# Group averages of the first norm: two matmuls with an averaging matrix, or block transposes and sums on VectorE

## Chip, cores and metric

The kernel runs on one core of a Trainium2 chip. The metric is the device time in microseconds (us) of one execution. Engines are named as in the profile: PE is TensorE (its weight loads are PEld), DVE is VectorE, ACT is ScalarE, POOL is GpSimd, and SP issues the DMAs.

## What is computed

The input is 32 images of 56 x 56 positions with 128 channels, float32. Two residual layers follow one another, each behind a group norm with 32 groups of four channels. Layer 0 is shifted-window attention (windows of 7 x 7, four heads), layer 1 a pair of truncated cosine transforms with a mixing matrix per mode and a feed-forward network (128 to 512 to 128).

```
def _gn(v, G=32, eps=1e-5):
    g = v.reshape(B_, H_, W_, G, C_ // G)
    m = mean(g, axis=(1, 2, 4));  s = var(g, axis=(1, 2, 4))
    return ((g - m) / sqrt(s + eps)).reshape(v.shape)

x = x + attention(_gn(x), rpb_table, w_qkv, w_proj, b_proj)
x = x + fourier_ff(_gn(x), w0, w1, W1, b1, W2, b2)
```

The change concerns the first `_gn` only. Its mean and variance run over all positions of an image and over the four channels of a group.

## The kernel before

Channels lie on the 128 partitions for the attention. An image is eight rows of windows (NWR = 8), and a row is one "cycle" of the main loop; a cycle takes about 14 us, an image about 112.5 us. Within a cycle the program issues, one after the other and in an order written by hand (`full_first`, then `quarters`, `attn_max`, `half_columns`, `eighths`, `full_last`), the pieces of three images: a row of attention of the present image, and the cosine transforms and the feed-forward groups of the one or two before. PE, ACT, DVE and POOL each execute their instructions strictly in that order; DMAs are issued by SP.

The statistics of the next image are prepared while the present one is still in attention. In cycles 4 to 6 of an image `next_image` calls `image_group` for the eight rows of the next image: PE transposes (L259), ACT copies the row (L269), DVE takes its per-channel statistics (L270), POOL adds the projection's bias to the residual (L274). After the three groups of cycle 6, `image_norm` starts. It is a generator that is advanced at four points: at the end of cycle 6, inside `full_first` of cycle 7, at the start of `full_last` of cycle 7, and at its end.

- Step 1: DVE aggregates mean and variance per channel (L281, `mv`).
- Step 2: PE multiplies the means by `gavg`, a 128 x 128 matrix with 0.25 in blocks of 4 x 4 (L284). DVE copies the group mean (L286), stores its negative as an extra column of the image's first row (L288), and forms e = (mean - group mean)^2 + variance (L290, L292).
- Step 3: PE averages e with the same matrix (L297), DVE adds 1e-5 (L299), POOL takes the power -1/2 (L301, `rstd`), DVE forms nb = -mean x rstd (L303).
- Step 4: ACT scales the projection weights by rstd (L308, `wn`), PE computes the bias of v (L310) and DVE copies it (L312). The next image's q and k matmuls (L321, L328) use `wn`.

Other lines that the text below speaks of: L429 copies half of the transposed attention weights from PSUM (DVE; the other half L427 is on ACT); L494 adds the projection to the residual and L508 and L517 sum it for the second norm (DVE); L333 on ACT and then L341 on DVE write the two halves of k for the scores L375 (PE); L405, L407 and L408 sum, invert and scale the softmax (DVE, DVE, POOL), L393, L394 and L400 take the maximum, subtract it and apply the exponential (DVE, POOL, ACT); L711, L719 and L731 are the feed-forward network (PE, ACT, PE), L701 adds its bias to the residual (POOL) and L740 adds the result (DVE). PSUM tiles of the attention rotate through four banks (`pa`), those of the second layer through four others (`pc`).

The part of `full_first` that sets the order around the second step of the norm:

```
attn_qk(im, i, False)          # L321, L328, then k on ACT and DVE
...
next(norm)                     # step 2
...
ff_in(im, FF_AT.index(c))      # L701, L711, L719
...
attn_divide(cycle - 1)         # L405, L407, L408
```

Of the kernel before, what the change touches and what calls it, by code (L numbers as in the profile page):

```python
# [10 lines left out]
F32 = mybir.dt.float32  # L11
AF = mybir.ActivationFunctionType
ALU = mybir.AluOpType
AX = mybir.AxisListType

P = 128
S = 56
C = 128
# [30 lines left out]
def swin_fourier_kernel(  # L49
# [20 lines left out]
    nc = tc.nc  # L70
    NB = x.shape[0]

    const = ctx.enter_context(tc.tile_pool(name="const", bufs=1))
    big = ctx.enter_context(tc.tile_pool(name="big", bufs=1))
    work = ctx.enter_context(tc.tile_pool(name="work", bufs=2))
    small = ctx.enter_context(tc.tile_pool(name="small", bufs=4))
# [3 lines left out]
    def bank(tag, bufs):  # L80
        return psum.tile([P, HB], F32, tag=tag, name=tag, bufs=bufs)

    def attn_bank():
        return bank("pa", 4)
# [38 lines left out]
    def const_load(shape, src, name):  # L123
        t = const.tile(shape, F32, tag=name, name=name)
        (nc.scalar if name in FIRST else nc.sync).dma_start(t, src)
        return t
# [9 lines left out]
    gavg = const_load([P, P], group_avg, "gavg")  # L136
# [11 lines left out]
    with nc.allow_non_contiguous_dma(reason="relative position bias, once"):  # L148
# [4 lines left out]
        for ix in range(WS):  # L153
            src = bass.AP(
                rpb_rev.tensor, rpb_rev.offset + WS - 1 - ix, [[span, NH * span], [1, WS]]
            )
# [41 lines left out]
    with nc.allow_non_contiguous_dma(reason="constant, once"):  # L198
        for blk in range(8):
# [4 lines left out]
            src = idct_h.rearrange("p (h r) -> p h r", r=4)[modes, :, 2 * li : 2 * li + 2]  # L204
# [47 lines left out]
    def image_group(im, i):  # L252
# [22 lines left out]
            piece, piece, bproj.unsqueeze(1).to_broadcast([TC, n1 - n0, C]), ALU.add  # L275
        )

    def image_norm(im):

        mv = small.tile([P, 2], F32, tag="mv", name="mv")  # L280
        nc.vector.bn_aggr(mv, im.st)  # L281
        yield
        pg = attn_bank()
        nc.tensor.matmul(pg[:, 0:1], lhsT=gavg, rhs=mv[:, 0:1], start=True, stop=True)  # L284
        gm = small.tile([P, 1], F32, tag="gm", name="gm")
        nc.vector.tensor_copy(gm, pg[:, 0:1])  # L286

        nc.vector.tensor_scalar(im.xw[0][:, RT : RT + 1], gm, -1.0, None, ALU.mult)  # L288
        d = small.tile([P, 1], F32, tag="d", name="d")
        nc.vector.tensor_tensor(d, mv[:, 0:1], gm, ALU.subtract)  # L290
        e = small.tile([P, 1], F32, tag="e", name="e")
        nc.vector.scalar_tensor_tensor(  # L292
            out=e, in0=d, scalar=d, in1=mv[:, 1:2], op0=ALU.mult, op1=ALU.add
        )
        yield
        pv = attn_bank()
        nc.tensor.matmul(pv[:, 0:1], lhsT=gavg, rhs=e, start=True, stop=True)  # L297
        ve = small.tile([P, 1], F32, tag="ve", name="ve")
        nc.vector.tensor_scalar(ve, pv[:, 0:1], 1e-5, None, ALU.add)  # L299
        rstd = small.tile([P, 1], F32, tag="rstd0", name="rstd0")  # L300
        nc.gpsimd.tensor_tensor(rstd, ve, mhalf, ALU.pow)  # L301
        nb = small.tile([P, 1], F32, tag="nb0", name="nb0")
        nc.vector.scalar_tensor_tensor(  # L303
            out=nb, in0=gm, scalar=-1.0, in1=rstd, op0=ALU.mult, op1=ALU.mult
        )
        im.w = work.tile([P, 3 * C], F32, tag="wn", name="wn")
        yield
        nc.scalar.mul(im.w, wqkv, rstd)  # L308
        pb = attn_bank()
        nc.tensor.matmul(pb[:, 0:1], lhsT=wqkv[:, 2 * C :], rhs=nb, start=True, stop=True)  # L310
        im.bias = small.tile([P, 5], F32, tag="bqkv", name="bqkv")
        nc.vector.tensor_copy(im.bias[:, 2:3], pb[:, 0:1])  # L312
        yield


# [597 lines left out]
    with tc.manual_schedule(engines={ET.PE, ET.Activation, ET.DVE, ET.Pool}):  # L913
        images[0] = image_begin(0)
        for i in range(NWR):
            image_group(images[0], i)
        for _ in image_norm(images[0]):
            pass
        norm = nothing()
        for cycle in range(NB * NWR + CONV_BEGIN + FF_AT[-1] - NWR + 1):  # L920
            if cycle < CONV_BEGIN:
                first_rows(cycle, norm)
            else:
                full_first(cycle, norm)
                if (cycle - CONV_BEGIN) % NWR != 3:
                    quarters(cycle)
                    if row(cycle)[0]:
                        attn_max(cycle)
                    half_columns(cycle)
                    eighths(cycle)  # L930
                else:
                    half_columns(cycle)
                    quarters(cycle)
                    eighths(cycle)
                    if row(cycle)[0]:
                        attn_max(cycle)
                full_last(cycle, norm)
            b, i = divmod(cycle, NWR)
            norm = nothing()
            if i == NWR - 2 and b + 1 < NB:  # L940
                norm = image_norm(images[b + 1])
                next(norm)
# [62 lines left out]
```

## Time and profile before

Three runs took 3694.38, 3694.4 and 3697.74 us.

| Engine or resource | Busy us | Share |
|---|---|---|
| PE | 3628.2 | 98% |
| PEld (overlaps PE) | 2966.3 | 80% |
| DVE | 2185.3 | 59% |
| ACT | 2151.0 | 58% |
| POOL | 1372.0 | 37% |
| DMA queue of SP | - | 37.6% of 16 engines |

The instructions of the norm, 32 times each (mean of one, in ns): L281 364, L286 150, L288 154, L290 181, L292 243, L299 150, L303 1120, L312 149 on DVE; L301 551 on POOL; L308 620 on ACT. A float32 matmul appears as two passes in the records, so L284, L297 and L310 have 64 entries each, of 214, 263 and 218 ns.

How to read it: PE's matmuls are pipelined and the records model their ends, so a busy PE need not be PE at its peak. A group's idle column tells how long its engine stood still just before it, and what released it. The timeline is in order of time and has the start, the duration and, in brackets, the idle time ahead.

### The profile page before, as it was taken

Reading aid. Unit: us, or ns where it says so; the run is one execution under the profiler, and the core shown is the slowest. Engines: PE = TensorE matmul, PEld = TensorE weight load, DVE = VectorE, ACT = ScalarE, POOL = GpSimd, SP = SyncE. Lnnn points to the kernel's source line nnn. Section 1 sums busy time; section 2 is a strip of 40 time slices with the busy share of each in tenths; the row PEclk is TensorE's granted clock in tenths of the full one; section 3 lists DMA queues with packets and bytes.
Section 4 is the critical chain, followed back from the end, with each engine's and each line's share of the span. In section 5 each row is a group of like instructions: output and inputs, shape, how many; then the busy total and the mean of one; then the engine's idle time right before and its main releaser. Section 6 shows DMA issues by size and latency. Waiting matters only on the chain.

```text
span 3694.8 us, 139935 instructions
## 1 busy us (share of the span) xinstructions
PE 3628.2 (98%) x61440; PEld 2966.3 (80%) x61440; DVE 2185.3 (59%) x4577; ACT 2151.0 (58%) x3915; POOL 1372.0 (37%) x1421
## 2 busy tenths in 40 slices
PE   6899999999999999999999999999999999999998
PEld 5678888888888887888888888878888888888886
DVE  6655666655665556665556656556655566565641
ACT  4555566655656655566556566555665565565553
POOL 5333343333334333433333343334333333433321
PEclk9999999999999999999999999999999999999999
DMA  4333434343434334334334344343344343333332
GB/s 112 93 102 104 116 93 109 107 111 101 113 95 114 108 105 113 96 105 110 108 102 113 95 111 108 105 113 100 101 112 108 101 115 97 108 107 106 95 107 89
DMA packets 687777, 388.93 MB, mean 105 GB/s; under 512 B 40479, under 2 KB 658112, under 8 KB 686912
## 3 DMA queue, kind: packets, MB, share of 16 engines
q1 hardware_dynamic: 686557, 379.65, 37.6%
q8 instruction: 484, 7.93, 0.9%
q14 instruction: 125, 1.02, 0.1%
q10 hardware_dynamic: 611, 0.32, 0.0%
HBM read 218.29 MB, written 161.48 MB: 103 GB/s over the span
## 4 chain that ended last, share of the span: by engine, by line
PE 93%; DVE 4%; DMA 1%; SPq 1%; ACT 1%; issue 0%; POOL 0%; ACTq 0%; POOLq 0%; DVEq 0%
PE pc L731 21%; PE pc L711 18%; PE pa L353 7%; PE pc L629 6%; PE pc L595 6%; PE pa L375 6%; PE pa L419 5%; PE pa L486 5%; PE pc L668 5%; PE pa L328 5%; PE pa L444 4%; PE pa L321 4%; PE pa L259 2%; DVE st L270 1%; DVE a L383 1%; DVE mx L393 1%
## 5 line engine op out<-in xcount | busy, mean ns | idle before, releaser
L408 POOL TENSOR_TENSOR a<-a,rs 128x784 f32<-128x784 f32 x256 | 389.9, 1523 | 1231.0 <-DVE rs L407 962.6
L731 PE MATMUL pc<-wff,hid 128*128 128x128 f32 (+1 forms) x6400 | 778.6, 279 | 0.9 <-ACT hid L719 0.7
L731 PEld LDWEIGHTS pc<-wff,hid 128*128 128x128 f32 (+1 forms) x6400 | 731.1, 189 | 21.1 <-issue 2.1
L711 PE MATMUL pc<-xf,wff 128*128 128x512 f32 (+2 forms) x1792 | 713.1, 540 | 0.9 <-ACT z L637 0.9
L719 ACT ACTIVATE hid<-pc,b1sb 128x512 f32<-128x512 f32 (+2 forms) x896 | 536.6, 635 | 97.8 <-PE pc L711 94.2
L711 PEld LDWEIGHTS pc<-xf,wff 128*128 128x128 f32 x1792 | 337.0, 190 | 301.7 <-issue 229.5
L394 POOL TENSOR_TENSOR a<-a,mx 128x784 f32<-128x784 f32 x256 | 389.4, 1521 | 451.6 <-DVE mx L393 450.4
L740 DVE TENSOR_TENSOR res<-pc,res 128x512 f32<-128x512 f32 (+2 forms) x256 | 143.6, 571 | 597.0 <-issue 273.9
L427 ACT COPY aT<-pa 113x452 f32<-113x452 f32 x256 | 137.8, 538 | 457.6 <-PE pa L419 457.5
L274 POOL TENSOR_TENSOR xl<-xl,bproj 112x384 f32<-112x384 f32 (+1 forms) x256 | 291.9, 1142 | 248.7 <-PE pa L259 248.7
L383 DVE TENSOR_TENSOR a<-pa,bm 128x392 f32<-128x392 f32 x512 | 259.6, 550 | 199.3 <-PE pa L375 199.1
L341 DVE TENSOR_SCALAR k<-pa,heads,bqkv 128x392 f32<-128x392 f32 x246 | 168.6, 685 | 275.3 <-ACT k L333 275.3
L475 DVE TENSOR_SCALAR oT<-pa,bqkv 128x98 f32<-128x98 f32 (+2 forms) x768 | 171.0, 279 | 266.4 <-PE pa L444 266.4
L400 ACT ACTIVATE a<-a 128x784 f32<-128x784 f32 x256 | 223.1, 872 | 168.9 <-POOL a L394 168.5
L360 ACT COPY v<-pa 128x512 f32<-128x512 f32 x256 | 152.9, 597 | 278.4 <-PE pa L353 278.4
L701 POOL TENSOR_TENSOR res<-res,b2sb 128x512 f32<-128x512 f32 (+2 forms) x256 | 263.5, 1035 | 101.4 <-DMA res<-scr 91.3
L375 PEld LDWEIGHTS pa<-k,q 64*64 64x64 f32 x8192 | 184.0, 132 | 137.8 <-DVE rs L407 68.2
L353 PE MATMUL pa<-wn,xw 128*64 128x128 f32 x4096 | 281.8, 280 | 3.7 <-DVE a L383 3.7
L353 PEld LDWEIGHTS pa<-wn,xw 128*64 128x64 f32 x4096 | 219.8, 137 | 51.6 <-issue 17.2
L393 DVE TENSOR_REDUCE mx<-a 128x16 f32<-128x784 f32 x256 | 247.6, 967 | 5.7
L405 DVE TENSOR_REDUCE sm<-a 128x16 f32<-128x784 f32 x256 | 245.9, 961 | 4.9 <-ACT a L400 4.9
L419 PE MATMUL pa<-ident,a 113*113 113x113 f32 x2048 | 248.2, 264 | 0.7 <-POOL a L408 0.7
(89 smaller groups left out, 5896.8 us busy)
## 6 DMA issues: line engine op xcount, KB each, us to landing
zscr<-z SPq DMA_DIRECT2D x512, 112.0 KB
htok<-scr SPq DMA_DIRECT2D x256, 196.0 KB
zT<-zscr SPq DMA_DIRECT2D x192, 256.0 KB
res<-scr SPq DMA_DIRECT2D x160, 256.0 KB
out_dram<-res SPq DMA_DIRECT2D x128, 256.0 KB
scr<-xl SPq DMA_DIRECT2D x128, 224.0 KB
xl<-in_x_dram SPq DMA_DIRECT2D x32, 784.0 KB
xl<-in_x_dram SPq DMA_DIRECT2D x32, 672.0 KB
```

The lines of the kernel that those rows point to most:

```text
L274: nc.gpsimd.tensor_tensor(piece, piece, bproj.unsqueeze(1).to_broadcast([TC, n1 - n0, C]), ALU.add)
L353: nc.tensor.matmul(pv[hs, j * C : (j + 1) * C], lhsT=im.xw[i][:, w * WT : w * WT + JP], rhs=im.w[:, 2 * C : 3 * C], start=True, stop=True,)
L375: nc.tensor.matmul(ps[hp][HALVES[e], pr * 2 * WT : (pr + 1) * 2 * WT], lhsT=q[cs, w * WT : w * WT + JP], rhs=k_sb[cs, :, w], start=True, s ...
L383: nc.vector.tensor_tensor(a[:, 2 * hp : 2 * hp + 2, :, 0:WT].rearrange("p u w j -> p w u j"), ps[hp][:, :RT].rearrange("p (w u j) -> p w u ...
L393: nc.vector.tensor_reduce(mx, a3, axis=AX.X, op=ALU.max)
L394: nc.gpsimd.tensor_tensor(a3, a3, mx.unsqueeze(2).to_broadcast([P, 2 * NWR, WT]), ALU.subtract)
L408: nc.gpsimd.tensor_tensor(a3, a3, rs.unsqueeze(2).to_broadcast([P, 2 * NWR, WT]), ALU.mult)
L419: nc.tensor.transpose(pt[:PW, h * P : h * P + PW], a[:PW, h, 2 * hf : 2 * hf + 2].rearrange("p w j -> p (w j)")[:, :PW], ident[:PW, :PW],)
L701: nc.gpsimd.tensor_tensor(res[:m, c0:c1], res[:m, c0:c1], b2sb[:m].unsqueeze(1).to_broadcast([m, c1 - c0, C]), ALU.add,)
L711: nc.tensor.matmul(ph[:, :n], lhsT=wff1[:, f * P : (f + 1) * P], rhs=xff[:, t0 : t0 + n], start=True, stop=True,)
L719: nc.scalar.activation(hf[:, :n], ph[:, :n], AF.Relu, bias=b1sb[:, f : f + 1])
L731: nc.tensor.matmul(pf[:m, c * C : (c + 1) * C], lhsT=im.hid[f][:, c * P : c * P + m], rhs=wff2[:, f], start=(f == 0), stop=(f == NF - 1),)
```

## The change

The two averages over groups of four channels leave PE. [...] So the aggregate now goes into the first two columns of a 128 x 32 tile `stat` that is zeroed once; a block transpose turns channels into columns (32 channels of each quarter of the partitions, mean in the first row of a block and variance in the second); `average` sums groups of four columns and spreads a quarter of the sum back over them. Deviations from the mean are squared and averaged in the same way (in the row of the means), and one block transpose of both results brings them back to one value per partition. The group variance is the sum of the averaged variances and the averaged squares. Everything of the norm up to nb is issued in one piece at the end of cycle 6; the weights' scaling and the bias matmul follow at the start of `full_last` of cycle 7. The two other points at which the generator is advanced now do nothing. `gavg` stays, since the second norm reads it (L545).

```diff
     def image_norm(im):
-        mv = small.tile([P, 2], F32, tag="mv", name="mv")
-        nc.vector.bn_aggr(mv, im.st)
-        yield
-        pg = attn_bank()
-        nc.tensor.matmul(pg[:, 0:1], lhsT=gavg, rhs=mv[:, 0:1], start=True, stop=True)
-        gm = small.tile([P, 1], F32, tag="gm", name="gm")
-        nc.vector.tensor_copy(gm, pg[:, 0:1])
+        GR = C // 16
+        def average(out, src):
+            sums = small.tile([P, GR], F32, tag="gsums", name="gsums", bufs=2)
+            nc.vector.tensor_reduce(
+                sums, src.rearrange("p (g c) -> p g c", c=4), axis=AX.X, op=ALU.add
+            )
+            nc.vector.tensor_scalar(
+                out.rearrange("p (g c) -> p g c", c=4),
+                sums.unsqueeze(2).to_broadcast([P, GR, 4]),
+                0.25,
+                None,
+                ALU.mult,
+            )
+        nc.vector.bn_aggr(stat[:, 0:2], im.st)
+        turned = small.tile([P, 32], F32, tag="turned", name="turned", bufs=2)
+        nc.vector.transpose(turned, stat)
+        mean = small.tile([P, 2, 32], F32, tag="gmeans", name="gmeans", bufs=2)
+        average(mean[:, 0], turned)
+        nc.vector.tensor_tensor(turned, turned, mean[:, 0], ALU.subtract)
+        nc.vector.tensor_tensor(turned, turned, turned, ALU.mult)
+        average(mean[:, 1], turned)
+        back = small.tile([P, 2, 32], F32, tag="back", name="back", bufs=2)
+        nc.vector.transpose(
+            back.rearrange("p k c -> p (k c)"), mean.rearrange("p k c -> p (k c)")
+        )
+        gm = back[:, 0, 0:1]
         nc.vector.tensor_scalar(im.xw[0][:, RT : RT + 1], gm, -1.0, None, ALU.mult)
-        d = small.tile([P, 1], F32, tag="d", name="d")
-        nc.vector.tensor_tensor(d, mv[:, 0:1], gm, ALU.subtract)
-        e = small.tile([P, 1], F32, tag="e", name="e")
+        ve = small.tile([P, 1], F32, tag="ve", name="ve")
         nc.vector.scalar_tensor_tensor(
-            out=e, in0=d, scalar=d, in1=mv[:, 1:2], op0=ALU.mult, op1=ALU.add
-        )
-        yield
-        pv = attn_bank()
-        nc.tensor.matmul(pv[:, 0:1], lhsT=gavg, rhs=e, start=True, stop=True)
-        ve = small.tile([P, 1], F32, tag="ve", name="ve")
-        nc.vector.tensor_scalar(ve, pv[:, 0:1], 1e-5, None, ALU.add)
+            out=ve, in0=back[:, 0, 1:2], scalar=1e-5, in1=back[:, 1, 0:1], op0=ALU.add, op1=ALU.add
+        )
         rstd = small.tile([P, 1], F32, tag="rstd0", name="rstd0")
         nc.gpsimd.tensor_tensor(rstd, ve, mhalf, ALU.pow)
...
         im.w = work.tile([P, 3 * C], F32, tag="wn", name="wn")
+        yield
         yield
         nc.scalar.mul(im.w, wqkv, rstd)
...
         nc.vector.tensor_copy(im.bias[:, 2:3], pb[:, 0:1])
+        yield
         yield
```

More of the change, by code (lines that the diff above doesn't have):

```diff
@@ L276, in image_group @@
         )
+    stat = const.tile([P, C // 4], F32, tag="stat", name="stat")
+    nc.vector.memset(stat, 0.0)
     def image_norm(im):
-        mv = small.tile([P, 2], F32, tag="mv", name="mv")
-        nc.vector.bn_aggr(mv, im.st)
-        yield
-        pg = attn_bank()
-        nc.tensor.matmul(pg[:, 0:1], lhsT=gavg, rhs=mv[:, 0:1], start=True, stop=True)
-        gm = small.tile([P, 1], F32, tag="gm", name="gm")
-        nc.vector.tensor_copy(gm, pg[:, 0:1])
+        GR = C // 16
[24 more added lines that the diff above has]
+        gm = back[:, 0, 0:1]
```

## The prediction

> **What bounds the kernel now.** I read the busy times of the page first, then the list of waits of the tensor engine (PE), then the timeline around one change of image, and last the stretches in which PE ran at half clock.
>
> ```profile
> PE 3628.2 (98%) x61440; PEld 2966.3 (80%) x61440; DVE 2185.3 (59%) x4577; ACT 2151.0 (58%) x3915; POOL 1372.0 (37%) x1421
> PE 93%; DVE 4%; DMA 1%; SPq 1%; ACT 1%; issue 0%; POOL 0%; ACTq 0%; POOLq 0%; DVEq 0%
> ```
>
> The first line is the busy time of each engine, the second the chain that ended last. PE is busy all the time and in order: whatever stops PE for a microsecond costs a microsecond, and whatever stops another engine costs nothing until PE has to wait for it. So there are two questions: how much PE time do the removed matmuls free, and does the longer VectorE (DVE) chain make PE wait?
>
> The groups of the norm (the first two columns after the bar are the total and the mean):
>
> ```profile
> L284 PE MATMUL pa<-mv,gavg 128*128 128x1 f32 x64 | 9.3, 214 | 3.0 <-DVE mv L281 1.7 <-ACT k L337 1.4
> L297 PE MATMUL pa<-e,gavg 128*128 128x1 f32 x64 | 12.4, 263 | 2.0 <-DVE e L292 2.0
> ```
>
> Both averages together keep PE busy 21.7 us, and PE waited only 5.0 us for them in the whole run. The averaging matmuls are cheap and hidden already. Now the timeline where the second half of the norm meets the next row of windows (start in us, duration, engine, line):
>
> ```profile
> 1853.26 1.27 POOL L274 TENSOR_TENSOR xl<-xl,bproj 112x512 f32<-112x512 f32 x1
> 1853.32 0.36 DVE L281 BATCH_NORM_AGGREGATE mv<-st 128x2 f32<-128x48 f32 x1
> 1853.60 0.57 DVE L429 COPY aT<-pa 113x452 f32<-113x452 f32 x1
> 1854.08 0.54 DVE L508 TENSOR_REDUCE part<-xl 112x32 f32<-112x384 f32 x1
> 1854.33 0.28 PE L284 MATMUL pa<-mv,gavg 128*128 128x1 f32 x2
> 1854.46 1.97 PE L711 MATMUL pc<-xf,wff 128*128 128x256 f32 x8
> 1854.49 0.72 POOL L701 TENSOR_TENSOR res<-res,b2sb 128x256 f32<-128x256 f32 x1
> 1855.30 0.69 DVE L341 TENSOR_SCALAR k<-pa,heads,bqkv 128x392 f32<-128x392 f32 x1 [0.68 <-ACT k L333]
> 1856.37 0.91 PE L375 MATMUL pa<-k,q 64*64 64x98 f32 x32
> ...
> 1862.81 0.55 POOL L301 TENSOR_TENSOR rstd<-ve,mhalf 128x1 f32<-128x1 f32 x1 [1.06 <-DVE ve L299]
> 1863.33 1.27 POOL L701 TENSOR_TENSOR res<-res,b2sb 128x512 f32<-128x512 f32 x1
> 1863.40 1.22 DVE L303 SCALAR_TENSOR_TENSOR nb<-gm,rstd 128x1 f32<-128x1 f32 x1 [0.66 <-POOL rstd L301]
> ```
>
> Right after the aggregate (L281) DVE does the copy L429, the sum L508 and then L341, which writes the second half of k. PE's scores (L375) need that k. L341 ends at 1855.99 and PE reaches L375 at 1856.37, so DVE has only 0.3 us to spare here, plus the 0.68 us that it waits for ScalarE: together 1.1 us. In 29 of the 31 changes of image the distance from L281 to L341 is 1.97 or 1.98 us and to L375 3.05 us, so one boundary stands for all. In another boundary (L341 at 169.10) PE did wait, and L375 then began at 169.84, 0.05 after L341's end.
>
> [...] L303 (two one-column inputs) lasts 0.16 us where nothing follows L301 on POOL, and here 1.22 us, to 1864.62, when POOL's L701 ends at 1864.60. [...] (PE busy is the first time after the length; the clock stands after the five engines):
>
> ```profile
> 128.31:131.72 3.41, 1.52 (x47) 1.42 (x48) 0.67 (x3) 1.39 (x3) 1.14 (x2) 1.00 0.80 227
> 131.72:135.13 3.41, 3.41 (x13) 2.56 (x12) 1.92 (x3) 0.79 (x2) 0.00 (x0) 0.50 0.32 76
> ...
> 155.61:159.03 3.42, 1.58 (x42) 0.95 (x45) 2.47 (x5) 2.32 (x5) 2.70 (x5) 1.00 0.66 191
> 159.03:162.44 3.41, 3.41 (x102) 3.26 (x96) 2.68 (x5) 2.46 (x5) 2.04 (x2) 1.00 0.36 101
> ```
>
> A window with 1.52 us of PE work was followed by one at half clock, a window with 1.58 us was not. So 1.86 us of idling within one window costs a window at half clock, about 1.6 us of PE work. [...]
>
> **The change part by part.** (a) *Matmuls away.* Per image, L284 and L297 go, and the bias matmul L310 moves up to the place of L297. Weight loads follow one another at 0.22 us per such pair there (L297's at 1861.86, the next line's at 1862.08; L310's at 1864.74, then 1864.96). L284 held PE 0.13 us (1854.33 to 1854.46), but its place lies just ahead of the wait below and gains nothing. Gain 0.22 us per image.
>
> (b) *DVE chain.* The whole chain, up to and with nb, now runs in one piece behind L281, ahead of L429, L508 and L341. Each step waits for the one before: steps of one column took 0.15 to 0.22 us with 0.04 between dependent ones (L286 to L288). For 32 elements I take 0.18 (add or multiply), 0.19 (sum: L556 takes 0.22 for 64), 0.22 and 0.25 for the transposes (0.15 to 0.45 each is possible). From the end of L281 at 1853.68: transpose to 1853.94, sum 1854.17, scale 1854.39; [...] square 1854.83, sum 1855.06, scale 1855.28, transpose back 1855.57, -mean 1855.76, ve 1855.85.
>
> (c) *The new wait.* rstd stays on POOL: 0.08 to hand over and 0.55, to 1856.48. nb on DVE waits for it. In POOL's new order L701 of this row stands right behind rstd (it was ahead of it); its data had landed by 1854.49, so it starts at once, 0.73 us, and shuts nb out until 1857.20. Behind nb on DVE stand L429, L508 and L341; PE's L375 waits for L341, with every later matmul behind it.
>
> (d) *Sum.* L429 starts 1857.12 (the next instruction starts 0.08 before nb's end, as after L303) instead of 1853.60: 3.52 later. L341 was free to start from 1854.54, so now 1858.06, ends 1858.75, and L375 starts at 1858.80 instead of 1856.37: 2.43 us later. PE idles from 1856.30 to 1858.80, 2.50 us. PE has no idle time worth naming later in the image in which to catch up (66 us in the whole run, most of it in the first 200 us).
>
> (e) *Half clock.* An idle stretch of 2.50 us puts 1.86 us into one window of 3.41 us unless the window's edge cuts it near its middle, which happens in (2 x 1.86 - 2.50)/3.41 = 36% of positions. So in 64% of images the next window runs at half clock: 0.64 x 1.6 = 1.0 us.
>
> (f) *Nothing:* wn (L308, 0.62 us on ScalarE) moves ahead of the exponentials L400, whose result is used a row later; the copies L286, L312 and the DVE steps that leave the end of the row stand where PE did not wait for DVE; gavg is still loaded. In the first image the chain meets POOL's additions L274 until 19.26, and nb would come near 19.9 as before (19.80): nothing.
>
> Per image 2.43 - 0.22 + 1.0 = 3.2 us, 31 times: 99.5 us; 3694.4 + 99.5 = 3794.
>
> **Rivals.** *The wait without the clock.* If idling of this length doesn't drop the clock, or the windows fall luckily, 2.2 x 31 = 68: 3762. For it: in the steady part no drop was ever seen; against it: five drops in the trace, all after such windows. *A gain.* If the tail of the norm is hidden (nb not shut out, L341 reaching PE in time), only matmuls vanish: 2 x 0.22 x 31 = 14 less, 3681. For it: PE 98% busy, DVE 59%. Against it: the chain adds 3.5 us where 1.1 us is free. *Longer steps.* With transposes of 0.45 us and the scalings shut out too, 0.6 us more per wait, and 85% of images dropping the clock: (2.8 + 1.4) x 31 = 130: 3824.
>
> **How the numbers follow.** Main case 60%, wait without clock 20%, longer 13%, gain 7% (of which 2% is no change). The range reaches from below the case without clock, with the shortest steps (1.8 x 31 = 56: 3750), to 3828, and leaves out the gain and the far tails. Slower 0.93, same 0.02, faster 0.05.
>
> **What would show it.** In the profile after: L375 waiting about 2.5 us for the k half on DVE, once per image, at the row after the aggregate; nb about 0.7 us long, ending with L701; windows of 3.41 us at clock 0.50 in the steady part, some 20 of them; PE busy not lower by more than 21 us except for the slowed matmuls. The prediction is wrong if DVE steps of 32 elements take much less than 0.15 us, [...] or if the clock stays at 1.00.

## The result and the profile after

The changed kernel takes 3798.9 us (3792.95 to 3800.43), the kernel before 3694.39 us (3692.93 to 3697.74): ratio 1.0278, 95% interval 1.0265 to 1.0291. It is slower by 104.5 us, 3.4 us for each of the 31 changes of image. Lines of the changed kernel are numbered anew from the norm on: 23 more than before (L341 is now L364, L375 is L398, L429 is L452, L701 is L724, L711 is L734, L731 is L754); in the norm itself L300 aggregates, L303 and L310 transpose, L289 sums, L292 scales, L322 is rstd, L324 nb, L332 the bias matmul.

First the page: the busy time of the engines and the chain that ended last.

```profile
PE 3642.4 (96%) x61312; PEld 2977.8 (79%) x61312; DVE 2220.9 (59%) x4738; ACT 2145.1 (57%) x3915; POOL 1370.9 (36%) x1421
PE 87%; DVE 6%; POOL 3%; issue 2%; DMA 1%; SPq 1%; ACT 1%; POOLq 0%; ACTq 0%; DVEq 0%
```

PE has 128 passes fewer and is nevertheless busy 14 us longer, while its share of the closing chain fell from 93% to 87%; DVE and POOL have moved into that chain. The list of PE's waits (the line that waits, the line waited for, then total, times and longest) names the place. The first line is the changed kernel, the second the same wait in the kernel before:

```profile
PE pa L398 <- DVE k L364: 91.4, 35, 4.1
PE pa L375 <- DVE k L341: 8.3, 6, 1.8
```

The timeline of one change of image in the changed kernel:

```profile
1904.92 1.27 POOL L274 TENSOR_TENSOR xl<-xl,bproj 112x512 f32<-112x512 f32 x1
1904.97 0.36 DVE L300 BATCH_NORM_AGGREGATE stat<-st 128x2 f32<-128x48 f32 x1
...
1905.37 0.21 DVE L303 STREAM_TRANSPOSE turned<-stat 128x32 f32<-128x32 f32 x1
...
1905.84 0.39 DVE L292 TENSOR_SCALAR gmeans<-gsums 128x32 f32<-128x32 f32 x1
1905.96 1.89 PE L734 MATMUL pc<-xf,wff 128*128 128x256 f32 x8
...
1906.93 0.18 DVE L292 TENSOR_SCALAR gmeans<-gsums 128x32 f32<-128x32 f32 x1
...
1907.50 0.15 DVE L318 SCALAR_TENSOR_TENSOR ve<-back 128x1 f32<-128x1 f32 x1
1907.73 0.55 POOL L322 TENSOR_TENSOR rstd<-ve,mhalf 128x1 f32<-128x1 f32 x1 [1.54 <-DVE ve L318]
1908.24 0.72 POOL L724 TENSOR_TENSOR res<-res,b2sb 128x256 f32<-128x256 f32 x1
1908.31 0.67 DVE L324 SCALAR_TENSOR_TENSOR nb<-back,rstd 128x1 f32<-128x1 f32 x1 [0.66 <-POOL rstd L322]
1908.90 0.62 DVE L452 COPY aT<-pa 113x452 f32<-113x452 f32 x1
1909.44 0.54 DVE L531 TENSOR_REDUCE part<-xl 112x32 f32<-112x384 f32 x1
1909.90 0.67 DVE L364 TENSOR_SCALAR k<-pa,heads,bqkv 128x392 f32<-128x392 f32 x1
1910.63 0.90 PE L398 MATMUL pa<-k,q 64*64 64x98 f32 x32 [2.77 <-DVE k L364]
```

The chain holds DVE's queue from 1904.97 to 1908.98, 0.66 us of it waiting for rstd. The copy, the sum and the k half stand behind it, and PE waits 2.77 us for the k half. nb ends with POOL's L724, as forecast (1908.98 and 1908.96). In the last 29 changes of image, called the steady part below, PE waits 2.77 or 2.78 us, and L398 starts 5.64 to 5.66 us behind the aggregate, 2.6 more than before.

The 51 changes of the granted clock in this trace lie whole multiples of 3.413 us apart; such stretches are called windows here. Two windows each from two images (PE busy is the first time after the length, the clock stands after the five engines):

```profile
1557.94:1561.36 3.42, 1.26 (x6) 0.76 (x4) 2.62 (x10) 2.18 (x6) 1.24 (x2) 1.00 0.33 91
1561.36:1564.77 3.41, 2.79 (x64) 2.80 (x68) 3.29 (x7) 0.00 (x0) 1.08 (x1) 0.50 0.00 0
1325.84:1329.25 3.41, 1.42 (x7) 0.92 (x5) 2.58 (x10) 2.55 (x6) 1.24 (x2) 1.00 0.35 102
1329.25:1332.67 3.42, 2.63 (x92) 2.48 (x94) 3.35 (x8) 0.92 (x2) 0.92 (x1) 1.00 0.02 5
```

In the first pair more of the wait fell into one window (1.26 us of PE work are left in it), and the next ran at half clock; in the second the window's edge cut more of it off (1.42 us of PE work), and the clock stayed. It dropped in 19 of the 29 steady images. An image without a drop is 2.60 us longer than before (median, from aggregate to aggregate), one with a drop 3.84 us.

### The profile page after: what moved, and what is told of

Its sections match the earlier page's. It is cut to its first block, busy times and chain, and to the rows that moved or that the text cites. A ratio compares the mean times of both kernels' runs of the same rounds, so it can differ in the third digit from the quotient of the medians.

```text
span 3793.0 us, 139780 instructions
## 1 busy us (share of the span) xinstructions
PE 3642.4 (96%) x61312; PEld 2977.8 (79%) x61312; DVE 2220.9 (59%) x4738; ACT 2145.1 (57%) x3915; POOL 1370.9 (36%) x1421
## 3 DMA queue, kind: packets, MB, share of 16 engines
q14 instruction: 128, 1.04, 0.1%
## 4 chain that ended last, share of the span: by engine, by line
PE 87%; DVE 6%; POOL 3%; issue 2%; DMA 1%; SPq 1%; ACT 1%; POOLq 0%; ACTq 0%; DVEq 0%
PE pc L754 20%; PE pc L734 16%; PE pa L376 7%; PE pa L398 6%; PE pc L652 6%; PE pc L618 6%; PE pc L691 5%; PE pa L467 4%; PE pa L442 4%; PE pa L509 4%; PE pa L351 4%; PE pa L344 4%; POOL xl L274 2%; PE pa L259 1%; DVE st L270 1%
## 5 line engine op out<-in xcount | busy, mean ns | idle before, releaser
L754 PE MATMUL pc<-wff,hid 128*128 128x128 f32 (+1 forms) x6400 | 778.3, 279 | 0.9 <-ACT hid L742 0.7
L754 PEld LDWEIGHTS pc<-wff,hid 128*128 128x128 f32 (+1 forms) x6400 | 731.0, 190 | 21.0 <-issue 1.9
L734 PE MATMUL pc<-xf,wff 128*128 128x512 f32 (+2 forms) x1792 | 710.6, 539 | 0.0
L734 PEld LDWEIGHTS pc<-xf,wff 128*128 128x128 f32 x1792 | 339.7, 190 | 308.9 <-issue 230.2
L417 POOL TENSOR_TENSOR a<-a,mx 128x784 f32<-128x784 f32 x256 | 389.0, 1520 | 454.3 <-DVE mx L416 453.1
L274 POOL TENSOR_TENSOR xl<-xl,bproj 112x384 f32<-112x384 f32 (+1 forms) x256 | 291.0, 1138 | 248.7 <-PE pa L259 244.5
L398 PEld LDWEIGHTS pa<-k,q 64*64 64x64 f32 x8192 | 195.1, 139 | 227.4 <-DVE k L364 117.9
L498 DVE TENSOR_SCALAR oT<-pa,bqkv 128x98 f32<-128x98 f32 (+2 forms) x768 | 171.1, 279 | 301.2 <-PE pa L467 301.2
L398 PE MATMUL pa<-k,q 64*64 64x98 f32 x8192 | 246.8, 259 | 98.4 <-DVE k L364 91.4
L364 DVE TENSOR_SCALAR k<-pa,heads,bqkv 128x392 f32<-128x392 f32 x246 | 168.1, 684 | 248.3 <-ACT k L356 248.3
L724 POOL TENSOR_TENSOR res<-res,b2sb 128x512 f32<-128x512 f32 (+2 forms) x256 | 263.8, 1036 | 99.8 <-DMA res<-scr 89.6
```

Of the source, the lines that this page charges most:

```text
L274: nc.gpsimd.tensor_tensor(piece, piece, bproj.unsqueeze(1).to_broadcast([TC, n1 - n0, C]), ALU.add)
L398: nc.tensor.matmul(ps[hp][HALVES[e], pr * 2 * WT : (pr + 1) * 2 * WT], lhsT=q[cs, w * WT : w * WT + JP], rhs=k_sb[cs, :, w], start=True, s ...
L417: nc.gpsimd.tensor_tensor(a3, a3, mx.unsqueeze(2).to_broadcast([P, 2 * NWR, WT]), ALU.subtract)
L724: nc.gpsimd.tensor_tensor(res[:m, c0:c1], res[:m, c0:c1], b2sb[:m].unsqueeze(1).to_broadcast([m, c1 - c0, C]), ALU.add,)
L734: nc.tensor.matmul(ph[:, :n], lhsT=wff1[:, f * P : (f + 1) * P], rhs=xff[:, t0 : t0 + n], start=True, stop=True,)
L754: nc.tensor.matmul(pf[:m, c * C : (c + 1) * C], lhsT=im.hid[f][:, c * P : c * P + m], rhs=wff2[:, f], start=(f == 0), stop=(f == NF - 1),)
```

## The experiments

The theory: the chain costs because it stands on DVE between PE and the k half, and its idle stretch costs PE's clock besides. The rivals: DVE's added work costs wherever it stands; POOL's rstd is not part of it; the half-clock windows are chance.

### PE kept busy while it waits

```diff
     def quarters(cycle):
         im, i = row(cycle)
+        if im and i == NWR - 1 and cycle < (NB - 1) * NWR:
+            fill = conv_bank()
+            for n in (HB, HB, HB // 2):
+                nc.tensor.matmul(
+                    fill[:, :n], lhsT=wff1[:, :P], rhs=wff1[:, :n], start=True, stop=True
+                )
```

> The changed kernel with three matmuls of unused results (two of 512 columns, one of 256, some 2.2 us in all) ahead of the scores in cycle 7, in the place where PE waits. Theory (PE's idle stretch drops the clock in two images of three): idle falls to about 0.6 us per image, no window at half clock in the steady part, L398 starts as late as in the changed kernel; only the wait is left, 2.6 x 31 = 81 us less a little: 3770 to 3776 us, although PE does more work. Rival (the half-clock windows have another cause, or cost nothing): 3799 us or more.

Measured 3765.22 us, ratio 1.0193 (1.0176 to 1.0210); the kernel before took 3693.15 us beside it. The filled place in the timeline:

```profile
1888.39 2.42 PE L868 MATMUL pc<-wff 128*128 128x512 f32 x6
...
1891.29 0.90 PE L398 MATMUL pa<-k,q 64*64 64x98 f32 x32 [0.48 <-DVE k L364]
```

L398 starts 5.65 us behind the aggregate (1885.64) as in the changed kernel, PE idles 0.48 us instead of 2.77, and no window of the steady part runs at half clock. With 2.4 us of useless matmuls in every image the kernel is 34 us faster than without. So of the 104 us lost, some 72 stay when the clock holds, and some 32 go with it. Not all of the 32 lie in the steady part: in the profiled runs the changed kernel takes 25 us longer than the filled one from the fourth aggregate to the last (3249.16 against 3223.90 us) and 8 us longer ahead of that, where it has 30.7 us at half clock in the first 200 us and the filled one 10.2.

### nb out of the way

```diff
-        nc.vector.scalar_tensor_tensor(out=nb, in0=gm, scalar=-1.0, in1=rstd, ...)
         im.w = work.tile([P, 3 * C], F32, tag="wn", name="wn")
         yield
         yield
+        nc.vector.scalar_tensor_tensor(out=nb, in0=gm, scalar=-1.0, in1=rstd, ...)
```

> The changed kernel with nb alone moved to the start of full_last, so that DVE does not wait for POOL's rstd ahead of the k half. Theory: the wait of 0.66 us and the 0.67 us of nb leave the path, L398 starts 1.33 us earlier and waits 1.4 us; an idle stretch of 1.4 us drops no clock; about (2.6 - 1.3) x 31 = 40 us over before: 3735 us. Rival (the chain of small DVE steps is the cost, the wait for POOL is hidden): 3790 to 3799 us. Rival (the clock drops after short stretches too): 3765 us, with windows at half clock in the steady part.

Measured 3755.91 us, ratio 1.0168 (1.0153 to 1.0183): faster than the changed kernel by 43 us, but 21 us above the forecast. PE's waits tell both:

```profile
PE pa L398 <- DVE k L364: 51.7, 34, 3.2
PE pa L332 <- DVE nb L327: 35.3, 32, 8.1
```

The wait for the k half is 1.44 us, as expected, with no half-clock window in the steady part. But the bias matmul L332 stands at the start of `full_last`, right behind the attention's matmuls, and nb now comes there behind DVE's copies of their result: about 0.9 us per image that the theory had overlooked.

### nb with one tensor input

```diff
-        nc.vector.scalar_tensor_tensor(
-            out=nb, in0=gm, scalar=-1.0, in1=rstd, op0=ALU.mult, op1=ALU.mult
-        )
+        nc.vector.tensor_scalar(nb, gm, rstd, -1.0, ALU.mult, ALU.mult)
```

In the changed kernel nb, with two tensors, lasts 0.67 us, to the end of POOL's L724. The theory is that it would not do so with one.

> The changed kernel with nb formed by an operation that has one SBUF tensor and takes rstd as a per-partition scalar, instead of two SBUF tensors. Theory [...]: nb lasts 0.16 us instead of 0.67, L398 waits 2.26 us; 57% of images drop the clock: (2.1 + 0.57 x 1.3) x 31 = 88 us over before: 3782 us. Rival (nb is long for another reason, such as reading a fresh result of POOL): nb stays 0.67 us and the time 3799 us.

Measured 3793.57 us, ratio 1.0265 (1.0250 to 1.0280). Lines behind nb stand two higher than in the changed kernel (L398 is L396 here).

```profile
1908.17 0.72 POOL L722 TENSOR_TENSOR res<-res,b2sb 128x256 f32<-128x256 f32 x1
1908.24 0.21 DVE L324 TENSOR_SCALAR nb<-back,rstd 128x1 f32<-128x1 f32 x1 [0.66 <-POOL rstd L322]
...
1910.10 0.90 PE L396 MATMUL pa<-k,q 64*64 64x98 f32 x32 [2.31 <-DVE k L362]
```

nb lasts 0.21 us while POOL's L722 runs beside it to 1908.89, and the wait shrank by 0.46 us: for nb, the form with one tensor does not wait for POOL's addition and that with two does. That the number of tensors decides in general is not shown: the scaling L292, with one, lasts 0.38 us in this trace, to 1906.16, where POOL's L274 ends at 1906.13, and 0.18 us where POOL stands still. The time followed by 5 us only, which is within the noise of the two, where 0.46 us in 31 images would be 14. The clock now dropped in 23 of the 29 steady images (79%, not the 57% forecast), and an image with a drop was 1.56 us longer than one without (medians), so that the drops took back about 12 us: 23 of 1.56 against 19 of 1.24. In 18 of the 23 the window ahead of the drop has nearly the same PE time, 1.09 to 1.11 us: an image with a drop lasts close to 34 windows (median 116.17 us, 34 windows are 116.05), so that the next wait meets the window in nearly the same position. Taking all positions as equally likely was wrong here.

### The chain behind the k half

```diff
         nc.vector.bn_aggr(stat[:, 0:2], im.st)
+        yield
         ...                                   # transposes, sums, ve, rstd in full_first
-        nc.vector.scalar_tensor_tensor(out=nb, in0=gm, scalar=-1.0, in1=rstd, ...)
         im.w = work.tile([P, 3 * C], F32, tag="wn", name="wn")
         yield
-        yield
+        nc.vector.scalar_tensor_tensor(out=nb, in0=gm, scalar=-1.0, in1=rstd, ...)
```

> The same DVE chain as in the changed kernel, but only the aggregate stays at the end of cycle 6; the transposes, sums, ve and rstd stand behind the k half (L364) in cycle 7, nb at the start of full_last. Theory (the chain costs because it stands between PE and the k half): L398 starts about 3.0 us after the aggregate again, the clock stays at 1.00 in the steady part, and the two averaging matmuls are saved: 0.2 to 0.4 us per image, 3681 to 3688 us. Rival A (the added 1 to 2 us of DVE work per image cost wherever they stand): 3725 to 3760 us. Rival B (the moved weight scaling, bias matmul and PSUM rotation cost): still near 3799 us.

Measured 3760.94 us, ratio 1.0184 (1.0167 to 1.0201): as expected at L398, which starts 2.81 us behind the aggregate (1886.63 to 1889.44), and wrong in the sum:

```profile
1894.92 1.51 POOL L417 TENSOR_TENSOR a<-a,mx 128x784 f32<-128x784 f32 x1 [0.37 <-DVE mx L416]
1895.65 0.80 DVE L327 SCALAR_TENSOR_TENSOR nb<-back,rstd 128x1 f32<-128x1 f32 x1
...
1896.50 0.38 PE L332 MATMUL pa<-nb,wqkv 128*128 128x1 f32 x2 [1.50 <-DVE nb L327]
```

nb stands behind DVE's three copies L498 and then lasts 0.80 us, to 1896.45, where POOL's L417 ends at 1896.43; the bias matmul, moved up by the change, waits 1.50 us for it, and 17 images of the steady part drop the clock there. Rival B, as it had been put, has the place right (the moved bias matmul), though not its cause in the changed kernel itself, where nb was long done at that point.

So the bias matmul and wn go back to the end of the row:

```diff
+        yield
         nc.scalar.mul(im.w, wqkv, rstd)
         pb = attn_bank()
         nc.tensor.matmul(pb[:, 0:1], lhsT=wqkv[:, 2 * C :], rhs=nb, start=True, stop=True)
         ...
         yield
-        yield
```

> As the kernel with the chain behind the k half, but wn and the bias matmul go back to the end of full_last, behind the feed-forward and projection matmuls, as before the change; nb stays at the start of full_last. Theory (the 1.50 us that PE waited for nb there, and the half-clock windows after it, were all that was lost): no wait at the bias matmul, no half-clock window in the steady part, the two averaging matmuls are saved, 0.46 us per image: 14 us less than before, 3679 us. Rival (the added DVE work costs in some other place of the row): 3700 us or more.

Measured 3687.32 us against 3694.03 before, ratio 0.9980 (0.9972 to 0.9988): faster than the kernel before by 0.2%, which is clear of the noise but half of the forecast, and faster than the changed kernel. In the steady part PE no longer waits at either place. At the k half:

```profile
1854.56 0.68 DVE L364 TENSOR_SCALAR k<-pa,heads,bqkv 128x392 f32<-128x392 f32 x1 [0.66 <-ACT k L356]
...
1855.41 0.90 PE L398 MATMUL pa<-k,q 64*64 64x98 f32 x32
```

The transposes and sums on DVE are the same as in the changed kernel. Where they stand, with nb, wn and the bias matmul put behind them in time, is worth 112 us.

### What the matmuls were worth

```diff
-        pg = attn_bank()
-        nc.tensor.matmul(pg[:, 0:1], lhsT=gavg, rhs=mv[:, 0:1], start=True, stop=True)
-        nc.vector.tensor_copy(gm, pg[:, 0:1])
+        nc.vector.tensor_copy(gm, mv[:, 0:1])
...
-        nc.tensor.matmul(pv[:, 0:1], lhsT=gavg, rhs=e, start=True, stop=True)
-        nc.vector.tensor_scalar(ve, pv[:, 0:1], 1e-5, None, ALU.add)
+        nc.vector.tensor_scalar(ve, e, 1e-5, None, ALU.add)
```

> The kernel before without the two averages: the per-channel mean and e are used as if they were group values, so L284 and L297 and nothing else leave. It measures what their absence is worth on PE. From the weight-load spacing: 0.22 us each, 0.44 per image: 14 us less than before, 3679 us. From the busy time of both groups (21.7 us): 3671 us. If the waits around them counted: less than 3668 us.

Measured 3684.19 us, ratio 0.9974 (0.9963 to 0.9986): 10 us, with the interval from 5 to 14. That is about all there was to gain, and the kernel with the chain behind the k half and the bias last has 7 of it.

### How much DVE time is free ahead of the k half

On the kernel with the bias last, steps of unused results behind the aggregate:

```diff
+        nc.vector.tensor_scalar(pad[:, 0:31], gavg[:, 0:31], stat[:, 0:1], None, ALU.mult)
+        for _ in range(1):                     # 4 in the longer one
+            nc.vector.tensor_reduce(pad[:, 31:32], pad[:, 0:31], axis=AX.X, op=ALU.add)
+            nc.vector.tensor_scalar(pad[:, 0:31], gavg[:, 0:31], pad[:, 31:32], None, ALU.mult)
```

> As the kernel with the bias last, with three small DVE steps of unused results (0.65 us in all) behind the aggregate, ahead of the copy, the sum and the k half. Theory: L364 waited 0.66 us for ScalarE there and PE came 0.1 us after it, so up to 0.77 us is free: the same time as without the steps (3679 us, within 4). Rival (DVE time ahead of the k half counts in full): 20 us more, 3699 us.

> The same with nine such steps (2.0 us in all). Theory: 2.0 less the free 0.77 makes PE wait 1.25 us per image, too short for the clock to drop: 39 us more than without the steps, 3718 us, no half-clock window in the steady part. Rival (DVE time counts in full): 62 us more, 3741 us. Rival (DVE is hidden at 59% busy): 3679 us.

Measured 3705.43 us (1.0029, 1.0017 to 1.0040) and 3785.73 us (1.0246, 1.0232 to 1.0260), 18 and 98 us more than without them: both above the theory. The steps were longer than meant, since the first lasts 0.85 us, to 1859.06, beside POOL's L274, which ends at 1859.02; the same operation on the sum (L305, at 1859.31) takes 0.24 us with POOL standing still (short steps; L369 is the k half and L403 the scores here):

```profile
1857.74 1.28 POOL L274 TENSOR_TENSOR xl<-xl,bproj 112x512 f32<-112x512 f32 x1
1858.21 0.85 DVE L302 TENSOR_SCALAR pad<-gavg,stat 128x31 f32<-128x31 f32 x1
...
1861.20 0.91 PE L403 MATMUL pa<-k,q 64*64 64x98 f32 x32 [0.51 <-DVE k L369]
```

Taken by what they really put ahead of the copy (its start behind the aggregate's, less the 0.28 us of the kernel before), these five kernels lie on one line:

| Kernel | Copy behind the aggregate | DVE time put ahead | PE waits | Difference |
|---|---|---|---|---|
| short steps | 1.66 us | 1.38 us | 0.51 us | 0.87 us |
| nb later | 2.59 us | 2.31 us | 1.44 us | 0.87 us |
| long steps | 3.15 us | 2.87 us | 1.99 us | 0.88 us |
| nb, one input | 3.45 us | 3.17 us | 2.31 us | 0.86 us |
| as changed | 3.93 us | 3.65 us | 2.77 us | 0.88 us |

The first 0.87 us cost PE nothing, and every further microsecond is a microsecond of waiting. The rival of work that counts in full falls, and so does that of work that is hidden because DVE is busy 59%. The longer steps also dropped the clock, in 17 steady images, which the theory had excluded for a wait of the 1.25 us meant; the wait came to 1.99 us.

## Why the prediction was right

The time was forecast at 3794 and is 3799, with the mechanism named. By its own steps:

- (a) The matmuls' worth: forecast 0.22 us per image here and 14 us for both. Without the averages the kernel gains 10 us; in the changed kernel the gain is inside the scatter of the images (those without a drop are 1.4 to 2.9 us longer than before) and not seen by itself.
- (b) The chain: forecast to reach ve's end 2.17 us behind L281's; it took 2.32 (1905.33 to 1907.65). Transposes took 0.21 and 0.25 (forecast 0.22 and 0.25, the author's estimate, since the trace before holds none), sums 0.19, adds and multiplies 0.19. One step was wrong: the first scaling L292 takes 0.39 us instead of 0.18. It, and not the subtraction behind it (0.19), lasts until L274 ends (1906.19; L292 ends at 1906.23). The same step without L274 beside it takes 0.18, and in the first image it takes 1.20 beside L274. Why this step waits for POOL, and nb with one tensor does not, was not shown. The prediction had put a lengthened scaling into a rival; it belongs into the main case.
- (c) The wait for rstd and nb's lasting to the end of L724 came as forecast: 0.66 us, then 0.67 us. The kernel with one tensor input shows nb at 0.21 us beside the same addition, the kernel with nb later that the whole 1.33 us was on PE's path.
- (d) L398 came later by 2.43 us in the forecast, by 2.61 measured (5.66 us behind the aggregate here, 3.05 before): 3.65 us were put ahead of the copy instead of 3.52, and 1.04 of them were free instead of 1.09. PE idled 2.77 us instead of 2.50. That is more than L398 came late, because PE, with L284's 0.13 us gone, is ready for it 2.89 us behind the aggregate, where it had been 3.05; so the free time of the table above, which counts PE's waiting, is 0.87.
- (e) The clock: forecast 64% of images at 1.6 us, or 1.0 us per image; measured 66% (19 of 29) at 1.24 us, or 0.8 us per image. That the share came out so close is partly luck. Two sizes were off against each other: the idle time that drops the clock here is about 2.0 us of a window's 3.41, an estimate from the PE work of the windows ahead of the drops (it fell after windows with up to 1.40 us of PE work and stayed from 1.40 us on; with the long steps it fell up to 1.43), not 1.86, but the wait was longer too, and with both measured sizes the sum, 1 - (2 x 2.0 - 2.77)/3.41, gives 64% again. The two windows from which 1.86 was read are not alike: the one that dropped held 39 small matmuls (L444, 0.59 of its 1.52 us), the other none, a difference that the last section takes up. The sum also takes all positions in a window as equally likely, which failed with the one-input nb. The filled kernel's 32 us, where 31 had been forecast, agree in part by luck as well, since 8 us of the difference lie ahead of the steady part.
- (f) What was taken at nothing stayed at nothing in the steady part: PE does not wait for wn there, nor the bias matmul L332 for nb. In the first image it was not quite nothing: nb starts at 20.96 us and not near 19.9, since L292, L306 and L307 each lasted until one of POOL's additions L274 ended, or up to 0.1 us longer (1.20, 0.92 and 1.23 us, where they take 0.18, 0.19 and 0.19 without L274 beside them), and the first q matmul L344 starts at 21.68 us where L321 had started at 20.53.

By image, the wait of 2.6 us and the clock's 0.8 make up the 3.4 measured. The forecast reached 3.2 with a shorter wait, a dearer clock and a gain of 0.22 that does not show, so the close total is in part these errors cancelling. The rival of the wait without the clock stands at 3762 and is what the filled kernel measures (3765).

## What to carry to other kernels

An engine that is busy 59% of the time can still hold up the one that is busy 98%: before work is moved to it, look at the instruction that stands next in its queue and at how long the bound engine can go on without that one. Here the same chain costs 104 us ahead of the k half and gains 7 us behind it, with nb, wn and the bias matmul moved as well. A chain that is moved has to be finished before its own reader comes up: the first attempt only carried the wait to the bias matmul. And a wait of PE can cost more than its length: here those of 1.99, 2.31 and 2.77 us were followed by half-clock windows in most of the steady images, the one of 1.44 us in none, and one of 1.50 us behind small matmuls in 17. With waits of 0.51 us the mean granted clock of a run was 0.994 to 0.996, like the kernel before beside it (0.994 to 0.998), where the changed kernel had 0.985 to 0.988.

## What the runs showed beside this

The clock did not follow the busy time of the records alone. With the chain behind the k half, a window with more PE work than those of the changed kernel was followed by a drop:

```profile
1893.45:1896.86 3.41, 1.91 (x83) 1.60 (x80) 2.67 (x6) 2.48 (x5) 3.04 (x3) 1.00 0.40 135
1896.86:1900.28 3.42, 3.42 (x18) 3.42 (x18) 0.16 (x1) 0.48 (x1) 0.80 (x1) 0.50 0.26 77
```

That window holds the attention's small matmuls (L467, 49 x 32 weights and 49 columns), that of the changed kernel large ones (L734, 128 x 128 weights and 256 columns). In the same kernel a window with equal PE work was not followed by a drop:

```profile
514.46:517.88 3.41, 1.91 (x42) 1.77 (x29) 1.58 (x6) 2.00 (x4) 2.75 (x2) 1.00 0.41 135
517.88:521.29 3.41, 3.41 (x26) 2.90 (x25) 2.24 (x4) 0.92 (x3) 0.00 (x0) 1.00 0.42 119
```

It holds only 28 of the records of L467; nearly all of the rest is the large L754. Of the 27 steady windows with 1.81 to 2.03 us of PE work, 18 hold 54 or all 64 of L467, and 17 of these were followed by a drop; 9 hold at most 29, and none was. That the small matmuls are the cause is the author's estimate from these windows and the two of the prediction; no run tried it by itself, and the wait lies later in the windows that dropped. And in the kernel with the one-input nb, image and clock window fell into step and the same drop came image after image, which made a shorter wait nearly as dear as the longer one.
